# Graph attention scores: four row tiles of 32 rows instead of two of 64, with a plain key tile and a second mask buffer

## The chip, the cores and the metric

The kernel runs on one core of one Trainium2 chip. The time is that of the device for one execution, in microseconds (us), as the median of several runs. The engines are named as in the profile: PE is TensorE (matmul), PEld its weight loads, DVE is VectorE, ACT is ScalarE, POOL is GpSimd, SP is SyncE, which here only issues DMA transfers.

## The reference

128 graphs of 128 nodes with 256 features go through two layers. The first is a graph attention layer (two rounds of attention over neighbours), a layer norm, a feed-forward part of width 1024 with relu and a second norm. The second layer is the one that the change touches: attention with 8 heads of 32 features, in which each relation of the adjacency matrix has its own values.

```python
q = (src @ Wq + bq).reshape(Bb, Nn, h, dh).transpose(0, 2, 1, 3)
k = (src @ Wk + bk).reshape(Bb, Nn, h, dh).transpose(0, 2, 1, 3)
scores = jnp.einsum('bhid,bhjd->bhij', q, k) / np.sqrt(dh)
attn = jax.nn.softmax(scores, axis=-1)
out = jnp.zeros_like(q)
for r in range(Wv.shape[0]):
    v_r = (src @ Wv[r] + bv[r]).reshape(Bb, Nn, h, dh).transpose(0, 2, 1, 3)
    mask = (adj_matrix == r)[:, None]
    out = out + jnp.einsum('bhij,bhjd->bhid', attn * mask, v_r)
attn_out = out.transpose(0, 2, 1, 3).reshape(Bb, Nn, Dm) @ Wo + bo
x = _ln(src + attn_out, g1, beta1)
ff = jax.nn.gelu(x @ W1 + b1, approximate=False) @ W2 + b2
return _ln(x + ff, g2, beta2)
```

Everything is in fp32. The adjacency matrix of the inputs holds zeros and ones only, so two of the four relations occur.

## The kernel before, in words

The 128 graphs are worked on in 32 groups of 4 (`G`). A group goes through five stages: `load`, `gat` (the first layer's attention), `ff0` (its feed-forward part), `att` (the second layer's attention) and `ff1`. Each stage is a Python generator that yields planned durations; `layers` keeps the stages of several groups in a heap by due time, so that the work of neighbouring groups is interleaved. This order of emission is fixed on TensorE from planned time 280 on, and on SP's queue throughout (`kept`). [...]Two versions of all stages are built: `GENERAL` for any adjacency matrix, and `BINARY` for zeros and ones. A test at the start of the run chooses; with these inputs it is `BINARY`.

In `attention`, queries and keys of a whole group come from TensorE as 128x512 tiles (lines 468 and 474), for each of two halves of the features (`DC` = 2); 128 features are four heads of 32 (`HC` = 4). DVE writes the queries to `qT`. The keys go to a tile `kbd` that holds each key twice, in two column blocks. A column of ones and zeros (`c.own`) is the scale of the ACT instruction, and zeroes in each block the 32-row strips of every other head (line 476):

```python
for q in range(2):
    nc.scalar.activation(c.kbd[i][:, :, q], p, AF.Identity, scale=c.own[:, q:q + 1],
                         bias=c.bk_own[q][:, i:i + 1])
```

So one product over 64 rows (two heads) and 256 columns gives the scores of both heads. `weights(b)` makes for graph `b` four such products (line 490), in two row tiles of the array, into two banks of PSUM with four heads each. Then, for each bank: DVE takes the maxima (line 496), ACT the four exponentials with their sums (line 500), DVE the reciprocals (line 501), POOL scales (line 502). `turned(b)` transposes the result: DVE transposes 32x32 blocks (line 288), SP issues four DMA writes to `zd` (line 291) and one read back to `eT` (line 293); the features of a stage take the same way. `by_relation` multiplies `eT` with the mask into `m` (line 515, DVE), `values` makes `v` (lines 531 and 532), `weighted` takes the products of `eT` and `m` with `v` into `av` (line 544) in four column tiles, and line 577 applies `wo`.

In a group the scores of graphs 0 and 1 are emitted ahead of the loop over graphs, those of 2 and 3 inside it, after `weighted`. In the order on TensorE, the scores of graph 1 follow those of graph 0 with only one `av` product of the group before between them.

[...]Seven serve all tiles named `mm` (`bufs["mm"]` = 7), among them the score tiles; one serves `av`. Which bank a tile gets is settled when the program is built, and a product into a bank waits until the last reader of the tile before is done.

The other lines that matter: 333 and 378 are the products of the two halves of a feed-forward part, 346 to 360 the ACT, DVE and POOL steps between them, 403 to 407 the row of the first attention that goes out and back by DMA (`zs`, `zsd`), 435 to 454 the products of that attention.

Of the kernel before, what the change touches and what calls it, by code (L numbers as in the profile page):

```python
# [12 lines left out]
F32 = mybir.dt.float32  # L13
I32 = mybir.dt.int32
U32 = mybir.dt.uint32
AF = mybir.ActivationFunctionType
OP = mybir.AluOpType
AX = mybir.AxisListType
# [6 lines left out]
P = 128  # L25
G = 4
Q = 32
# [17 lines left out]

BINARY = dict(
    binary=True, times=TIMES,
    period=100, bufs=dict(T=5, tok=5, m=1, mm=7, v=2),
    begin=dict(load=-87, gat=-51, ff0=48, att=132, ff1=300),
    early={  # L50
        (1, "ff0"): 48,
# [34 lines left out]
def constants(tc, a, c, cst, tmp, ps):  # L86

    nc = tc.nc
    D, DC, R, MW = c.D, c.DC, c.R, c.MW
    T = G * P  # L90
    c.ident = cst.tile([P, P], F32, name="ident")
    make_identity(nc, c.ident)
    c.mhalf = cst.tile([P, G], F32, name="mhalf")
    nc.vector.memset(c.mhalf, -0.5)

    def wload(name, t=None):

        k, m = a[name].shape
        if t is None:
            t = cst.tile([P, k // P, m], F32, name=name)  # L100
        nc.sync.dma_start(t, a[name].rearrange("(c p) m -> p c m", p=P))
        return t

    def on_all_rows(first, n):

        v = a["rows"]
        return bass.AP(tensor=v.tensor, offset=v.offset + first * D, ap=[[0, P], [1, n * D]])

    c.xt, c.at = [], []

    def load_group(g):
        c.xt.append(tmp.tile([P, DC, T], F32, name=f"xt{g}"))
        nc.sync.dma_start(c.xt[g], a["xT"][g])

    def load_mask(g):
        c.at.append(tmp.tile([P, G, P], I32, name=f"at{g}"))
        nc.sync.dma_start(c.at[g], a["adjT"][g])

    m = wload("M", tmp.tile([P, DC, MW], F32, name="m_in"))
    w2T = wload("W2T", tmp.tile([P, DC, D], F32, name="w2T"))  # L120
    load_group(0)
    w1T = wload("W1T", tmp.tile([P, DC, D], F32, name="w1T"))
    load_mask(0)
    load_group(1)
    load_mask(1)

    pa = ps.tile([P, DC, 2], F32, name="mm")
    for kc in range(DC):
        for oc in range(DC):
            nc.tensor.matmul(pa[:, kc], w2T[:, oc, ts(kc, P)], m[:, oc, D:D + 2], start=oc == 0, stop=oc == DC - 1)  # L130
    nc.vector.tensor_copy(m[:, :, D:D + 2], pa)
    c.wx = cst.tile([P, DC, MW], F32, name="wx")
    for fc in range(DC):
        p = ps.tile([P, MW], F32, name="mm")
        for kc in range(DC):
            nc.tensor.matmul(p, w1T[:, kc, ts(fc, P)], m[:, kc], start=kc == 0, stop=kc == DC - 1)
        nc.vector.tensor_copy(c.wx[:, fc], p)

    for g in range(LEAD):
        nc.sync.dma_start(c.y[g], a["x"][g])  # L140
    col = cst.tile([P, a["cols"].shape[1]], F32, name="col")
    nc.sync.dma_start(col, a["cols"])
    c.col = {k: col[:, i:i + n] for k, (i, n) in COLS.items()}
    c.wf1 = wload("wf1")

    def others():

        ln_rows = cst.tile([P, len(KS), 2, D], F32, name="ln_rows")
        nc.sync.dma_start(ln_rows, on_all_rows(0, 8))
        plus = tmp.tile([P, 3, D], F32, name="plus")  # L150
        nc.sync.dma_start(plus, on_all_rows(8, 3))
        nc.vector.tensor_add(ln_rows[:, :3, 1], ln_rows[:, :3, 1], plus)
        c.ln = {k: (ln_rows[:, n, 0], ln_rows[:, n, 1]) for n, k in enumerate(KS)}
        c.wf2 = wload("wf2")
        c.wq = wload("wq")
        c.wk = wload("wk")
        c.wv = wload("wv")
        c.bv = cst.tile([P, R * D], F32, name="bv")
        nc.sync.dma_start(c.bv, on_all_rows(11, R))
        c.wo = wload("wo")  # L160
        c.w1 = wload("w1")
        c.w2 = wload("w2")
        c.kbd = [cst.tile([P, G, 2, P], F32, name=f"kbd{n}") for n in range(DC)]
        c.own = cst.tile([P, 2], F32, name="own")
        nc.vector.memset(c.own, 0.0)
        for q in range(P // Q):
            nc.vector.memset(c.own[ts(q, Q), q % 2:q % 2 + 1], 1.0)
        c.bk_own = [cst.tile([P, DC], F32, name=f"bk{q}") for q in range(2)]
        c.sums = {n: [cst.tile([P, w.shape[-1] // 2], F32, name=f"{n}s{i}") for i in (1, 2, 4)]
                  for n, w in (("wf1", c.wf1), ("w1", c.w1))}  # L170

    return others
# [43 lines left out]
def per_row(v, n):  # L216

    return v[:, :, None].to_broadcast([P, v.shape[-1], n])


def stages_of(tc, a, out, c, pools, plan):

    nc = tc.nc
    TIMES, binary = plan["times"], plan["binary"]
    ld, wk, sm, ps, dr = pools.ld, pools.wk, pools.sm, pools.ps, pools.dr
    x, xT, adjT = a["x"], a["xT"], a["adjT"]
    NG, N, _, D = x.shape
    assert N == P
    T = G * N
    NQ = N // Q  # L230
    DC, R, MW = c.DC, c.R, c.MW
    FC = a["wf1"].shape[1] // P
    H = 8
    DH = D // H
    HC = P // DH
# [223 lines left out]
    def attention(y, g, first, direct):  # L459
# [4 lines left out]
        qT = t_tile().rearrange("p (c t) -> p c t", c=DC)  # L464
        for i in range(DC):
            p = ps.tile([P, T], F32, name="mm")
            for f in range(DC):
                nc.tensor.matmul(p, c.wq[:, f, ts(i, P)], hT[:, :, f], start=f == 0, stop=f == DC - 1)  # L468
            nc.vector.tensor_scalar(qT[:, i], p, c.col["bq"][:, i:i + 1], SCALE, op0=OP.add, op1=OP.mult)

        for i in range(DC):
            p = ps.tile([P, G, N], F32, name="mm")
            for f in range(DC):
                nc.tensor.matmul(p, c.wk[:, f, ts(i, P)], hT[:, :, f], start=f == 0, stop=f == DC - 1)  # L474
            for q in range(2):
                nc.scalar.activation(c.kbd[i][:, :, q], p, AF.Identity, scale=c.own[:, q:q + 1],
                                     bias=c.bk_own[q][:, i:i + 1])

        if not binary:
            adj = ps.tile([P, G, N], F32, name="adj", bufs=1)  # L480
# [2 lines left out]
        def weights(b):  # L483


            scores = [ps.tile([P, DC, 2, N], F32, name="mm") for _ in range(2)]
            for i in range(DC):
                for h in range(2):
                    rows = ts(h, P // 2)
                    nc.tensor.matmul(scores[h][:, i], qT[rows, i, ts(b, N)], c.kbd[i][rows, b],  # L490
                                     start=True, stop=True, tile_position=(h * P // 2, 0))
            e = wk.tile([P, H, N], F32, name="e1")
            for h, p in enumerate(scores):
                p = p.rearrange("p c q n -> p (c q) n")
                nm = sm.tile([P, HC], F32, name="nm1")
                nc.vector.tensor_reduce(nm, p, AX.X, OP.max, negate=True)  # L496
                s = sm.tile([P, HC], F32, name="s1")
                eh = e[:, ts(h, HC)]
                for q in range(HC):
                    nc.scalar.activation(eh[:, q], p[:, q], AF.Exp, bias=nm[:, q:q + 1], accum_out=s[:, q:q + 1])  # L500
                nc.vector.reciprocal(s, s)  # L501
                nc.gpsimd.tensor_mul(eh, eh, per_row(s, N))  # L502
            return e

        def turned(e):
# [30 lines left out]
        def weighted(ms, v):  # L536

            po = ps.tile([P, DC, N], F32, name="av", bufs=1)

            order = range(RV) if binary else range(RV - 1, -1, -1)  # L540
            for i in range(DC):
                for n, r in enumerate(order):
                    for q in reversed(range(HC)):
                        nc.tensor.matmul(po[ts(q, DH), i], v[:, r, i * P + q * DH:i * P + (q + 1) * DH],  # L544
                                         ms[r][:, q // 2 * HC + i * 2 + q % 2],
                                         start=n == 0, stop=n == RV - 1, tile_position=(0, q * DH))
            oT = wk.tile([P, DC, N], F32, name="oT")
            nc.scalar.copy(oT, po)
            return oT
# [12 lines left out]
        v, ms = values(0), by_relation(0, eT[0], range(R))  # L562
# [36 lines left out]
def layers(ctx: ExitStack, tc: tile.TileContext, a: dict, out: bass.AP, c, plan: dict):  # L599
# [21 lines left out]
    def stage_attention(g):  # L621
        if g == 0:
            folded(nc, c, pools.ps, c.wq, c.col["bq"], "02")
            folded(nc, c, pools.ps, c.wk, c.col["bk"], "02")
            for q in range(2):
                nc.vector.tensor_scalar(c.bk_own[q], c.col["bk"], c.own[:, q:q + 1], None, op0=OP.mult)
            folded(nc, c, pools.ps, c.wv, c.bv, "02", rows=True)
            if plan["binary"]:
                D = c.D
                nc.vector.tensor_sub(c.wv[:, :, D:2 * D], c.wv[:, :, D:2 * D], c.wv[:, :, :D])  # L630
                nc.vector.tensor_sub(c.bv[:, D:2 * D], c.bv[:, D:2 * D], c.bv[:, :D])
            folded(nc, c, pools.ps, c.w1, c.col["b1"], "11")
            c.w1_sums = weight_sums(nc, c, c.w1, "w1")
        x2[g] = yield from attention(x1.pop(g), g, g == 0, g == NG - 1)
# [148 lines left out]
```

## Time and profile before

| | |
|---|---|
| median of 3 runs | 2890.71 us (2889.82 to 2892.4) |
| the profiled execution's own time | 2891.83 us |
| its span | 2890.0 us |
| mean TensorE clock granted | 0.982 |
| TensorE busy | 2787.7 us, 96% |
| ACT, POOL, DVE busy | 60%, 55%, 52% |
| scores on TensorE (L490) | 1024 records, 147.7 us busy |
| keys on ACT (L476) | 128 instructions, 92.6 us |
| exponentials on ACT (L500) | 1024 instructions, 362.1 us, with 242.9 us of reading the sums |
| maxima on DVE (L496) | 256 instructions, 162.9 us, 676 ns each |

A row of the profile names line, engine, operation, `out<-in` by the program's names, the shapes, how many there were, the busy time and the mean of one, and then the idle time of the engine ahead of it and what ended it. An fp32 product is two passes, so it shows as two records. Records of TensorE that start 7 ns apart run at the same time in different tiles of the array.

### The profile page before, as it was taken

The numbers are of one execution on the slowest core, as the hardware profiler recorded it, in microseconds if no ns is written. First come the engines' busy times: TensorE is split into PE (matmuls) and PEld (weight loads), VectorE is DVE, ScalarE is ACT, GpSimd is POOL, SyncE is SP. The second block draws the span as 40 slices with busy tenths as digits, with TensorE's granted clock in tenths as the row PEclk, the third lists the DMA queues.
The fourth block names the chain that finished last, engine by engine and source line by source line (L and its number), as shares of the span: only waits on it lengthen the run. The fifth ranks groups of instructions, "written<-read, shape, count | busy, mean of one in ns | idle before, by whom it ended". The sixth has DMA issues, their size and how long they took to land.

```text
span 2890.0 us, 45554 instructions
## 1 busy us (share of the span) xinstructions
PE 2787.7 (96%) x15554; PEld 2166.1 (75%) x15554; DVE 1504.7 (52%) x3072; ACT 1724.3 (60%) x5191; POOL 1597.4 (55%) x1866
## 2 busy tenths in 40 slices
PE   4996999999999999999999999999999999999988
PEld 3764777777877777777777787777778777777756
DVE  5444545545545555554554555555565545555442
ACT  3445566566666666666656666666666675666543
POOL 1434556556655556665655665565566565556553
PEclk7998999999999999999999999999999999999999
DMA  7145454555554556555445545454654544564310
GB/s 275 45 104 121 104 118 106 110 132 127 119 114 107 113 117 139 114 119 118 106 108 131 129 113 125 104 111 117 137 128 107 123 106 111 122 135 106 77 37 15
DMA packets 1156945, 328.69 MB, mean 114 GB/s; under 512 B 903008, under 2 KB 1126752, under 8 KB 1156064
## 3 DMA queue, kind: packets, MB, share of 16 engines
q1 hardware_dynamic: 1156704, 325.68, 49.1%
q8 instruction: 126, 2.06, 0.3%
q14 instruction: 115, 0.94, 0.1%
HBM read 195.97 MB, written 129.62 MB: 113 GB/s over the span
## 4 chain that ended last, share of the span: by engine, by line
PE 71%; DMA 7%; DVE 6%; POOL 5%; ACT 4%; issue 2%; SPq 2%; DVEq 0%; POOLq 0%; ACTq 0%
PE mm L378 25%; PE mm L333 19%; PE mm L531 5%; PE mm L474 4%; PE mm L468 4%; PE mm L490 4%; PE av L544 3%; PE mm L435 3%; PE mm L577 3%; POOL tok L271 2%; DMA zd<-e 2%; SPq L291 2%; DMA eT<-zd 2%; PE mm L454 1%; DMA zd<-T 1%
## 5 line engine op out<-in xcount | busy, mean ns | idle before, releaser
L271 POOL TENSOR_TENSOR tok<-tok,ln_rows 128x512 f32<-128x512 f32 (+1 forms) x596 | 669.5, 1133 | 34.4 <-PE mm L282 11.1
L500 ACT ACTIVATE e<-mm,nm 128x128 f32<-128x128 f32 x1024 | 362.1, 397 | 239.2 <-DVE nm L496 229.6
L378 PE MATMUL mm<-w,fT 128*128 128x256 f32 x2048 | 460.6, 381 | 0.0
L378 PE MATMUL mm<-wf,fT 128*128 128x256 f32 x2048 | 456.6, 381 | 1.5 <-ACT fT L354 1.5
L378 PEld LDWEIGHTS mm<-w,fT 128*128 128x128 f32 x2048 | 386.6, 190 | 74.2 <-issue 24.2
L502 POOL TENSOR_TENSOR e<-e,s 128x512 f32<-128x512 f32 x256 | 269.4, 1053 | 300.5 <-DVE s L501 299.8
L378 PEld LDWEIGHTS mm<-wf,fT 128*128 128x128 f32 x2048 | 386.5, 190 | 64.3 <-issue 9.2
L515 DVE TENSOR_TENSOR m<-eT,am 128x1024 f32<-128x1024 f32 x128 | 186.2, 1454 | 385.2 <-DMA eT<-zd 374.8
L496 DVE TENSOR_REDUCE nm<-mm 128x4 f32<-128x512 f32 x256 | 162.9, 676 | 254.6 <-PE mm L490 254.6
L265 ACT ACTIVATE tok<-tok,nmr,rstd 128x256 f32<-128x256 f32 x480 | 249.9, 603 | 20.1 <-POOL nmr L263 20.0
L531 PE MATMUL mm<-wv,T 128*128 128x512 f32 x512 | 249.3, 610 | 0.0
L352 POOL TENSOR_TENSOR fT<-fT 128x512 f32<-128x512 f32 x128 | 163.3, 1277 | 153.8 <-ACT fT L351 153.8
L500 ACT ACTIVATION_READ_ACCUMULATOR e<-mm,nm 128x1 f32 x1024 | 242.9, 237 | 0.0
L354 ACT ACTIVATE fT<-fT,col 128x512 f32<-128x512 f32 x256 | 170.4, 715 | 118.8 <-DVE fT L348 117.1
L309 POOL TENSOR_TENSOR t<-T 128x256 f32<-128x256 f32 x64 | 47.6, 744 | 321.3 <-DMA T<-zd 321.0
L333 PE MATMUL mm<-T,w 128*128 128x256 f32 x768 | 202.3, 386 | 4.0 <-DMA T<-zd 2.9
L424 POOL TENSOR_TENSOR e<-e,s 128x512 f32<-128x512 f32 (+1 forms) x68 | 68.1, 1002 | 244.4 <-DVE s L423 230.6
L333 PE MATMUL mm<-T,wf 128*128 128x256 f32 x768 | 193.1, 381 | 0.0
L256 DVE BATCH_NORM_STATS2 st<-tok 128x6 f32<-128x256 f32 x480 | 176.7, 409 | 2.4
L333 PEld LDWEIGHTS mm<-T,w 128*128 128x128 f32 x768 | 144.4, 192 | 30.6 <-issue 6.5
L422 ACT ACTIVATE e<-e,nm 128x128 f32<-128x128 f32 x256 | 101.6, 430 | 105.2 <-DVE nm L419 98.8
L333 PEld LDWEIGHTS mm<-T,wf 128*128 128x128 f32 x768 | 146.1, 191 | 21.7 <-issue 0.8
(144 smaller groups left out, 5147.1 us busy)
## 6 DMA issues: line engine op xcount, KB each, us to landing
zd<-e SPq DMA_DIRECT2D x496, 128.0 KB, 4.6
eT<-zd SPq DMA_DIRECT2D x124, 512.0 KB, 4.4
zd<-T SPq DMA_DIRECT2D x364, 128.0 KB, 3.5
T<-zd SPq DMA_DIRECT2D x91, 512.0 KB, 4.2
xt<-in_xT_dram SPq DMA_DIRECT2D x32, 512.0 KB, 5.0
e<-zsd SPq DMA_DIRECT2D x60, 256.0 KB, 3.3
tok<-in_x_dram SPq DMA_DIRECT2D x30, 512.0 KB
out_dram<-tok SPq DMA_DIRECT2D x29, 512.0 KB, 5.4
```

The source lines that it names most:

```text
L256: nc.vector.bn_stats(st, y[:, b])
L265: nc.scalar.activation(y[:, b], y[:, b], AF.Identity, bias=nmr[:, b:b + 1], scale=rstd[:, b:b + 1])
L271: engine.tensor_tensor(y[:, b:b + n], y[:, b:b + n], v[:, None, :].to_broadcast([P, n, D]), op)
L333: nc.tensor.matmul(p[:, i], win[k][:, ts(f0 + i, P)], hs[k], start=first and i == 0, stop=True, skip_group_check=True)
L352: nc.gpsimd.tensor_add(hi[:, :, 1], hi[:, :, 1], hi[:, :, 0])
L354: nc.scalar.activation(lo[:, i], lo[:, i], func, bias=bin_[:, f0 + i:f0 + i + 1])
L378: nc.tensor.matmul(ys[b // 2][:, b % 2], fT[f][:, ts(b, N)], wout[:, f], start=b % 2 == 0 and n == 0, stop=n == FC - 1, skip_group_check=True)
L496: nc.vector.tensor_reduce(nm, p, AX.X, OP.max, negate=True)
L500: nc.scalar.activation(eh[:, q], p[:, q], AF.Exp, bias=nm[:, q:q + 1], accum_out=s[:, q:q + 1])
L502: nc.gpsimd.tensor_mul(eh, eh, per_row(s, N))
L515: nc.vector.tensor_tensor(m, eT, at[:, b][:, None, :].to_broadcast([P, H, N]), OP.mult)
L531: nc.tensor.matmul(p, hT[:, b, f], wv[:, f, r:r + 2], start=f == 0, stop=f == DC - 1)
```

## The change

`kbd` and what belongs to it go. The keys are written once, with their bias, to a plain tile `kT` of the same layout as `qT`. The scores of a graph are eight products over 32 rows (one head) and 128 columns, in four row tiles, and each row tile writes to a bank of its own: four banks with two heads each instead of two with four. Maxima are taken for each bank; reciprocals and the scaling on POOL still for four heads at a time. The order of heads in `e` changes, and `weighted` reads it in the new order. In `BINARY` the mask product `m` has two buffers instead of one.

```diff
-    period=100, bufs=dict(T=5, tok=5, m=1, mm=7, v=2),
+    period=100, bufs=dict(T=5, tok=5, m=2, mm=7, v=2),
...
-        c.kbd = [cst.tile([P, G, 2, P], F32, name=f"kbd{n}") for n in range(DC)]
-        c.own = cst.tile([P, 2], F32, name="own")
-        nc.vector.memset(c.own, 0.0)
-        for q in range(P // Q):
-            nc.vector.memset(c.own[ts(q, Q), q % 2:q % 2 + 1], 1.0)
-        c.bk_own = [cst.tile([P, DC], F32, name=f"bk{q}") for q in range(2)]
...
+        kT = wk.tile([P, DC, T], F32, name="kT", bufs=1)
         for i in range(DC):
-            p = ps.tile([P, G, N], F32, name="mm")
+            p = ps.tile([P, T], F32, name="mm")
             for f in range(DC):
                 nc.tensor.matmul(p, c.wk[:, f, ts(i, P)], hT[:, :, f], start=f == 0, stop=f == DC - 1)
-            for q in range(2):
-                nc.scalar.activation(c.kbd[i][:, :, q], p, AF.Identity, scale=c.own[:, q:q + 1],
-                                     bias=c.bk_own[q][:, i:i + 1])
+            nc.scalar.activation(kT[:, i], p, AF.Identity, bias=c.col["bk"][:, i:i + 1])
...
-            scores = [ps.tile([P, DC, 2, N], F32, name="mm") for _ in range(2)]
+            scores = [ps.tile([P, DC, N], F32, name="mm") for _ in range(HC)]
             for i in range(DC):
-                for h in range(2):
-                    rows = ts(h, P // 2)
-                    nc.tensor.matmul(scores[h][:, i], qT[rows, i, ts(b, N)], c.kbd[i][rows, b],
-                                     start=True, stop=True, tile_position=(h * P // 2, 0))
+                for q in range(HC):
+                    rows = ts(q, DH)
+                    nc.tensor.matmul(scores[q][:, i], qT[rows, i, ts(b, N)], kT[rows, i, ts(b, N)],
+                                     start=True, stop=True, tile_position=(q * DH, 0))
             e = wk.tile([P, H, N], F32, name="e1")
-            for h, p in enumerate(scores):
-                p = p.rearrange("p c q n -> p (c q) n")
-                nm = sm.tile([P, HC], F32, name="nm1")
-                nc.vector.tensor_reduce(nm, p, AX.X, OP.max, negate=True)
-                s = sm.tile([P, HC], F32, name="s1")
-                eh = e[:, ts(h, HC)]
-                for q in range(HC):
-                    nc.scalar.activation(eh[:, q], p[:, q], AF.Exp, bias=nm[:, q:q + 1], accum_out=s[:, q:q + 1])
-                nc.vector.reciprocal(s, s)
-                nc.gpsimd.tensor_mul(eh, eh, per_row(s, N))
+            nm = sm.tile([P, H], F32, name="nm1")
+            s = sm.tile([P, H], F32, name="s1")
+            for h in range(2):
+                some = slice(h * HC, (h + 1) * HC)
+                for q in (2 * h, 2 * h + 1):
+                    nc.vector.tensor_reduce(nm[:, ts(q, DC)], scores[q], AX.X, OP.max, negate=True)
+                for q in (2 * h, 2 * h + 1):
+                    for i in range(DC):
+                        k = q * DC + i
+                        nc.scalar.activation(e[:, k], scores[q][:, i], AF.Exp, bias=nm[:, k:k + 1],
+                                             accum_out=s[:, k:k + 1])
+                nc.vector.reciprocal(s[:, some], s[:, some])
+                nc.gpsimd.tensor_mul(e[:, some], e[:, some], per_row(s[:, some], N))
...
-                                         ms[r][:, q // 2 * HC + i * 2 + q % 2],
+                                         ms[r][:, q * DC + i],
```

More of the change, by code (lines that the diff above doesn't have):

```diff
@@ L624, in stage_attention @@
             folded(nc, c, pools.ps, c.wk, c.col["bk"], "02")
-            for q in range(2):
-                nc.vector.tensor_scalar(c.bk_own[q], c.col["bk"], c.own[:, q:q + 1], None, op0=OP.mult)
             folded(nc, c, pools.ps, c.wv, c.bv, "02", rows=True)
```

## The prediction

> **What bounds the kernel now.** I read the shares of busy time first, then the table by stage, then the instructions of one group in order of time, and last the chain that ended last.
>
> The table by stage has, after the stretch, its length, then busy time (and instructions) of PE, weight loads, DVE, ACT and POOL, the clock, DMA share and GB/s:
>
> ```profile
> PE 2787.7 (96%) x15554; PEld 2166.1 (75%) x15554; DVE 1504.7 (52%) x3072; ACT 1724.3 (60%) x5191; POOL 1597.4 (55%) x1866
> ...
> 288.00:2760.00 2472.00, 2460.93 (x13887) 1919.25 (x13886) 1322.57 (x2705) 1544.53 (x4660) 1452.67 (x1684) 1.00 0.52 116
> ```
>
> From 288 to 2760 us TensorE is busy 99.6% of the time at full clock; ACT, DVE and POOL have 37% to 47% free. The groups follow each other there every 85.05 us (14 of 26), 85.2 us (7) or 85.7 to 85.8 us (5). So a microsecond that TensorE saves or loses in a group counts, unless something else takes its place. The start (0 to 288) and the end are different: PE is busy 219.7 of the first 288 us.
>
> Now the place that the change touches, TensorE, then ACT, then DVE around one pair of scores (start, length, line, operation):
>
> ```profile
> 1581.49 1.13 PE L490 MATMUL mm<-kbd,T 64*128 64x256 f32 x8
> 1582.56 0.42 PE L544 MATMUL av<-eT,v 128*32 128x128 f32 x8
> ...
> 1583.57 1.13 PE L490 MATMUL mm<-kbd,T 64*128 64x256 f32 x8
> 1584.63 0.70 PE L378 MATMUL mm<-w,fT 128*128 128x256 f32 x2
> ```
> ```profile
> 1583.38 0.37 ACT L500 ACTIVATE e<-mm,nm 128x128 f32<-128x128 f32 x1 [5.94 <-DVE nm L496]
> ...
> 1585.11 0.39 ACT L500 ACTIVATE e<-mm,nm 128x128 f32<-128x128 f32 x1
> 1585.36 0.23 ACT L500 ACTIVATION_READ_ACCUMULATOR e<-mm,nm 128x1 f32 x1
> ```
> ```profile
> 1582.66 1.29 DVE L496 TENSOR_REDUCE nm<-mm 128x4 f32<-128x512 f32 x2 [6.35 <-PE mm L490]
> ```
>
> One graph's scores hold TensorE for 1.06 us (1582.56 - 1581.49). Graphs 0 and 1 of a group stand almost back to back, with one `av` product (1.01 us) between. The exponentials of graph 0 start 1.89 us after its first product and go at 0.34 us each; the sixth is done at 1585.59.
>
> The chain, last. It leaves TensorE at 1507.55 and comes back at 1560.60:
>
> ```profile
> 1508.42 1.24 DVE e L288
> ...
> 1524.15 4.42 DMA zsd<-zs
> ...
> 1531.93 4.24 DMA zd<-T
> ...
> 1559.37 0.71 ACT fT L354
> 1560.08 0.48 ACT fT L346
> ...
> 1560.60 1.13 PE mm L333 x4
> ```
>
> Transposes go out and back by DMA, one round trip after the other in SP's queue[...]. I took, in all 26 steady groups, the time between the end of L346's copy and the product L333 that waits for it: 0.05 us in 11 groups, about 1.1 us in 4, 1.8 to 2.3 us in 11. So this second bound stands level with TensorE in 11 groups of 26 and just behind in the others. Between 1507.55 and 1560.60 lie the scores of graphs 2 and 3 (1523.96 and 1542.62); those of 0 and 1 lie outside.
>
> [...]two row tiles start 7 ns apart, and a block of scores costs 0.2 us more than its four passes of 0.216 us. [...]load time goes with the columns, not the rows; the trace agrees: 187 ns for 64x128 (L490) and 190 for 128x128, against 110 for 128x32 (L544). So rows of 32 make no load cheaper. [...]
>
> **The change part by part.**
>
> *Score products.* Four passes of 256 columns (two row tiles at a time) become four of 128 columns (four at a time). A 128-column pass takes 0.109 us in L544. So 4 x 0.109 + 0.20 = 0.64 us, 0.42 less per graph. [...]Not concurrent at all: 1.94. I take 0.64, since column tiles of this size do reach 0.109.
>
> *Banks.* Seven banks serve `mm`; two graphs now ask for eight. The changed kernel's list of instructions has the order on TensorE from 288 us on unchanged, and shows that graph 1's second, third and fourth tiles use the banks of graph 0's first, second and third, so they wait for graph 0's second, fourth and sixth exponential. Count from graph 0's first product. Its results come 0.42 us sooner: DVE starts at 1.17 - 0.42 = 0.75. A maximum over 128x256 takes 0.41 (L419 has that form), and an exponential now waits for its own bank's maximum alone: ACT starts at 0.75 + 0.41 + 0.04 = 1.20. The sixth exponential with its accumulator is done 2.21 after that (1585.59 - 1583.38): 3.41. TensorE takes 0.05 to notice (as at 1560.60) and then a block of 0.64: it is free at 4.10, where before it was at 3.14. The pair **loses 0.96 us**; 0.87 if the bank is free at the exponential itself[...]. All of TensorE's queue stands behind it: L378, then the step at 1507.55 + 85.2 from which the DMA chain starts. So it is paid in full.
>
> *Graphs 2 and 3.* Their banks are free a microsecond or more before: they save 2 x 0.42 = 0.84 us of TensorE, inside the stretch that the chain spans. In 11 of 26 groups TensorE would only wait longer for L346 and nothing is gained; in 15 it is.
>
> *Key tile.* Four activations of 0.774 us per group become two: 64 x 0.774 = 50 us less of ACT. Covered: they end 5 us before the scores (1576.1 against 1581.5).
>
> *Maxima.* 512 x 0.408 - 256 x 0.676 = 36 us more of DVE. For graphs 2 and 3 a wait for DMA follows on DVE (3.0 us ahead of L515 at 1550.65), which hides it; for the pair it is counted above. Were the cover gone, L347 would be 0.3 us late.
>
> *Second mask buffer.* DVE waits for it once in the run, 8.0 us between 140 and 310 us; elsewhere L515 waits for the DMA of eT. Nothing in the steady part. In the start it may give up to 8 us or, since TensorE waits for another DMA there (12 us at 228), nothing. There the pair stalls too, 2 to 5 us, in idle time mostly. I take +1, bounds -6 to +6, for start and end.
>
> *Orders.* ACT's and SP's are the same over a group; DVE's and POOL's have a few neighbours exchanged. On POOL t L309 now stands behind rstd L259, so POOL's run there ends about 1.1 us later; its next reader, the transpose of e, has 5.8 us to spare. Nothing.
>
> **The sum.** 29 turns: 11/26 of them at +0.96, 15/26 at +0.96 - 0.84 = +0.12, mean 0.48: +14 us, +1 for the ends: the profiled execution's 2891.8 becomes about 2907; it stands 1.1 above the median of the three runs, so 2906.
>
> **The rivals.**
> - *TensorE alone sets the time*: the chain gives way. 29 x 0.12 = +3.5: 2894. For it: 15 groups have slack. Against: 11 have none. Chance 0.15.
> - *The chain holds in every group*: 29 x 0.96 = +28: 2919. Chance 0.10.
> - *Row tiles do not run four at a time*: 0.88 us more per graph instead of 0.42 less, and later exponentials: about +4.5 us a group, 3020. Against: two do, and four column tiles do. Chance 0.05.
> - *The bank wait is not paid* (the other side): the three banks come free before graph 1 asks for them, 1.65 us after the start. Then the pair gains 0.84 and the group 0.84 + 0.84 x 15/26 = 1.32: 2852. It decides at the time of the sixth exponential: the time falls from a release before 2.9 us on, against 3.41 worked out above. For it: ACT and DVE stand idle 6 us ahead and start at once. Against: six exponentials take 2.2 us, so the first would have to start at 0.7 instead of 1.20. Chance 0.10.
> - The forecast, chance 0.60, 2894 to 2914 by its bounds.
>
> **How the numbers follow.** What a measurement of this kernel can tell from no change is 0.2%, 5.8 us. Slower by more: most of the forecast (0.54), all of the second and third rival: 0.69. Within: 0.06 of the forecast and most of the first rival: 0.19. Faster: the last rival, and a good outcome of the start: 0.12. The range 2887 to 2922 takes in the forecast and the first two; it leaves out 0.15 and some of the edges.
>
> **What would show it.** Right: score blocks of 0.64 us for graphs 0, 2 and 3; the second block of the pair stretched to about 2.4 us, TensorE waiting for exponentials in it; 4.1 us from graph 0's product to L378; groups every 85.2 to 86.1 us. Wrong: no wait on ACT inside the second block, blocks over 0.8 us, or groups at or under 85.0 us.

## The result, and the profile after

The changed kernel takes **2914.82 us** (median of 4 runs, 2913.89 to 2915.51); the kernel before took 2891.56 beside it (4 runs, 2889.82 to 2892.98). The ratio is 1.0081, interval 1.0063 to 1.0098: slower by 0.8%. The forecast was 2906, range 2887 to 2922. The profiled execution took 2914.78 us with a span of 2913.0, against 2891.83 and 2890.0, so 23.0 us have to be found in the traces.

First the page of the kernel after: busy time of each engine, the chain that ended last, and the rows of exponentials and maxima. Below it stands the chain that ended last in the kernel before.

```profile
PE 2795.1 (96%) x16578; PEld 2181.4 (75%) x16578; DVE 1512.2 (52%) x3321; ACT 1674.8 (57%) x5127; POOL 1594.7 (55%) x1866
...
PE 85%; ACT 3%; DVE 3%; DMA 3%; issue 2%; POOL 2%; SPq 1%; ACTq 0%; DVEq 0%; POOLq 0%
...
L495 ACT ACTIVATE e<-mm,nm 128x128 f32<-128x128 f32 x1024 | 361.2, 394 | 218.8 <-DVE nm L491 209.4
...
L491 DVE TENSOR_REDUCE nm<-mm 128x2 f32<-128x256 f32 x512 | 182.6, 411 | 245.8 <-PE mm L483 245.7
```
```profile
PE 71%; DMA 7%; DVE 6%; POOL 5%; ACT 4%; issue 2%; SPq 2%; DVEq 0%; POOLq 0%; ACTq 0%
```

ACT has lost 50 us of work and a block of scores that waits for nothing is shorter on TensorE (below), yet the kernel is longer: neither saving reached the end. A maximum over 256 columns takes 0.411 us, as assumed. TensorE's share of the chain went from 71% to 85% and that of DMA from 7% to 3%, so the place to look is TensorE.

The pair of scores in one group, TensorE, then ACT, then DVE (start, length, line, operation, number of passes, and in brackets the idle time before it and who ended it). A block of eight products is sixteen passes (L483 has 2048 records for 1024 products):

```profile
1588.63 0.73 PE L483 MATMUL mm<-kT,T 32*128 32x128 f32 x16
1589.29 0.43 PE L540 MATMUL av<-eT,v 128*32 128x128 f32 x8
...
1590.30 0.88 PE L483 MATMUL mm<-kT,T 32*128 32x128 f32 x4
1591.39 0.48 PE L483 MATMUL mm<-kT,T 32*128 32x128 f32 x2 [0.21 <-ACT e L495]
1592.09 0.71 PE L483 MATMUL mm<-kT,T 32*128 32x128 f32 x10 [0.21 <-ACT e L495]
1592.72 3.72 PE L372 MATMUL mm<-w,fT 128*128 128x256 f32 x16
```
```profile
1589.83 0.37 ACT L495 ACTIVATE e<-mm,nm 128x128 f32<-128x128 f32 x1 [6.01 <-DVE nm L491]
...
1591.56 0.39 ACT L495 ACTIVATE e<-mm,nm 128x128 f32<-128x128 f32 x1
1591.81 0.23 ACT L495 ACTIVATION_READ_ACCUMULATOR e<-mm,nm 128x1 f32 x1
```
```profile
1589.37 1.41 DVE L491 TENSOR_REDUCE nm<-mm 128x2 f32<-128x256 f32 x4 [4.46 <-PE mm L483]
```

The first block, free of waits, holds TensorE for 0.66 us (1589.29 - 1588.63; before 1.06). The second, with as many passes, takes 2.42 us (1592.72 - 1590.30): it waits twice for an exponential of the graph before. The brackets show only 0.21 us each, since the modelled ends of the products ahead cover the rest; the distance between the starts shows the wait. The sixth exponential ends at 1592.04 with its accumulator, and the next product starts at 1592.09.

The chain over the same group (start, length, what):

```profile
1504.81 0.23 ACT e L495
1505.04 0.04 issue
1505.09 0.71 PE mm L483 x10
...
1552.55 5.12 DMA eT<-zd
...
1567.21 0.48 ACT fT L340
1567.69 0.04 issue
1567.73 1.13 PE mm L327 x4
```

It now runs through the exponentials that free the bank (1504.81) and then along TensorE until 1552.53. Before, it left TensorE ahead of this stretch and came back 53 us later; here it is away for 15 us. The round trips by DMA have less say in this group than the prediction gave them.

The steady stretch, in the columns of the table by stage:

```profile
288.00:2730.00 2442.00, 2419.90 (x14509) 1895.11 (x14508) 1301.08 (x2887) 1467.77 (x4519) 1413.22 (x1640) 1.00 0.52 115
```

TensorE is busy 99.1% of it, 99.6% before. The clock is 1.00 when rounded, but not everywhere. Two groups, each with the stretch of 3.41 us in which the second block starts and the 3.41 us after it:

```profile
1245.69:1249.10 3.41, 2.98 (x28) 2.17 (x21) 1.61 (x7) 3.41 (x20) 2.15 (x3) 1.00 0.01 5
1249.10:1252.51 3.41, 3.41 (x10) 2.69 (x9) 2.73 (x7) 3.41 (x20) 1.52 (x2) 0.50 0.00 0
1590.43:1593.84 3.41, 2.98 (x21) 2.27 (x22) 1.61 (x8) 3.41 (x19) 3.41 (x5) 1.00 0.31 73
1593.84:1597.25 3.41, 3.41 (x18) 3.00 (x17) 3.16 (x8) 3.41 (x21) 1.40 (x2) 1.00 0.02 5
```
```profile
1248.25 5.41 PE L372 MATMUL mm<-w,fT 128*128 128x256 f32 x16
1253.49 1.03 PE L327 MATMUL mm<-T,wf 128*128 128x256 f32 x4
```

In the first group TensorE gets **half its clock** (0.50) from 1249.10 to 1252.51, and the sixteen passes of L372 last 5.24 us (1253.49 - 1248.25). Those at 1592.72 last 3.56 (the next line starts at 1596.28). That is 1.68 us that no wait shows. It happens in 5 of the 26 steady groups, and in none before. This was in no term of my sum.

Where the 23.0 us went, by the trace: the start -1.5, the 26 groups +19.3, the end +5.2. A group takes 85.98 us on the mean, against 85.24. Of the 19.3, 5.5 is the longer group without any other wait (85.26 against 85.05, so 26 x 0.21), 8.4 the five half-clock stretches (5 x 1.68), and the 5.4 that remain are other waits (10.2 after, 4.8 before). As far as the records show them, they are for the last steps of the DMA chain (L340, L341), with idle time in 12 cases after and in none before, and in four or five cases on each side for `v`. The end holds two more half-clock stretches, at 2686.1 and 2713.4 us; the kernel before has none there until 2801. At the same 1.68 us each, an estimate, they would be 3.4 of its 5.2 us.

### The profile page after: what moved, and what is told of

The parts are those of the page before. It is cut to its first block, busy times and chain, and to the rows that moved or that the text cites. A ratio compares the mean times of both kernels' runs of the same rounds, so it can differ in the third digit from the quotient of the medians.

```text
span 2913.0 us, 47820 instructions
## 1 busy us (share of the span) xinstructions
PE 2795.1 (96%) x16578; PEld 2181.4 (75%) x16578; DVE 1512.2 (52%) x3321; ACT 1674.8 (57%) x5127; POOL 1594.7 (55%) x1866
## 4 chain that ended last, share of the span: by engine, by line
PE 85%; ACT 3%; DVE 3%; DMA 3%; issue 2%; POOL 2%; SPq 1%; ACTq 0%; DVEq 0%; POOLq 0%
PE mm L372 31%; PE mm L327 24%; PE mm L527 7%; PE mm L462 4%; PE mm L469 4%; PE mm L573 3%; PE mm L483 3%; PE av L540 3%; PE mm L429 3%; ACT e L495 2%; PE mm L448 2%; PE mm L437 2%; DMA eT<-zd 1%; DMA zd<-e 1%; DVE nm L491 1%
## 5 line engine op out<-in xcount | busy, mean ns | idle before, releaser
L372 PE MATMUL mm<-w,fT 128*128 128x256 f32 x2048 | 471.2, 387 | 0.0
L372 PE MATMUL mm<-wf,fT 128*128 128x256 f32 x2048 | 458.2, 381 | 1.5 <-ACT fT L348 1.5
L372 PEld LDWEIGHTS mm<-w,fT 128*128 128x128 f32 x2048 | 393.4, 193 | 71.1 <-issue 14.5
L372 PEld LDWEIGHTS mm<-wf,fT 128*128 128x128 f32 x2048 | 384.4, 190 | 61.6 <-ACT fT L354 5.0
L491 DVE TENSOR_REDUCE nm<-mm 128x2 f32<-128x256 f32 x512 | 182.6, 411 | 245.8 <-PE mm L483 245.7
L253 POOL TENSOR_SCALAR rstd<-mv 128x4 f32<-128x4 f32 x129 | 32.0, 248 | 261.9 <-DVE mv L251 256.6
L382 DVE TENSOR_TENSOR tok<-tok,mm 128x512 f32<-128x512 f32 x120 | 81.5, 679 | 165.0 <-PE mm L372 165.0
```

Of the source, the lines that this page charges most:

```text
L372: nc.tensor.matmul(ys[b // 2][:, b % 2], fT[f][:, ts(b, N)], wout[:, f], start=b % 2 == 0 and n == 0, stop=n == FC - 1, skip_group_check=True)
L491: nc.vector.tensor_reduce(nm[:, ts(q, DC)], scores[q], AX.X, OP.max, negate=True)
```

## The experiments

Two theories. The **bank wait**: the second block waits for the exponentials because the two graphs ask for eight of seven banks, and that costs more than the row tiles save; half clock follows from the same wait. The **rivals**: the row tiles cost something themselves; or the second mask buffer, the key tile or the many small maxima do; or the DMA chain sets the time whatever TensorE saves.

**Later scores.** The scores of graph 1 stand behind eight more products of L372, so that exponentials have time; the next planned step (`turn0`) is shortened by as much, so that what follows keeps its planned time. Tiles, banks and counts stay.

```
-    binary=True, times=TIMES,
+    binary=True, times=TIMES | dict(scores=7, turn0=8.5),
```

> The changed kernel, with the scores of graph 1 emitted later in planned time (7 instead of 5.5), so that on TensorE eight products of the feed-forward part (3.5 us) stand between the av product and them; nothing else moves in a steady group. Theory (the cost is the wait of the pair for banks): the sixth exponential of graph 0 is done 3.41 us after its first product, graph 1 asks at 0.66 + 1.01 + 3.5 = 5.2 us, so no wait is left; four blocks of 0.66 us, groups every 83.5 us where the DMA chain does not hold and 84.3 where it does, and no stretch at half clock in the steady part: 2850 us (2840 to 2866). Rival (row tiles of 32, the smaller maxima or the DMA chain cost the time, not the wait): 2890 to 2915 us.

Measured: 2881.87 us (2876.0 to 2882.32), ratio to before 0.9957, interval 0.9943 to 0.9971. TensorE in one group:

```profile
1567.52 0.73 PE L483 MATMUL mm<-kT,T 32*128 32x128 f32 x16
...
1572.84 0.73 PE L483 MATMUL mm<-kT,T 32*128 32x128 f32 x16
1573.50 1.13 PE L327 MATMUL mm<-T,wf 128*128 128x256 f32 x4
...
1596.80 6.31 PE L372 MATMUL mm<-wf,fT 128*128 128x256 f32 x28 [0.35 <-ACT fT L354]
```

Both blocks of the pair now take 0.66 us, and between 288 and 2640 us no half clock is left: with the bank wait, both losses are gone. But the time is 32 us above what I expected, in neither range. A new wait for ACT (0.35 us in the last line, 0.5 to 0.6 us of TensorE's time) comes in nearly every group, since ACT does graph 1's exponentials later; that they are what delays it is read from the trace, not tested. Waits of other kinds come back in nine or ten groups. A typical group takes 84.34 us, the mean 84.73. About half of what was set free was taken by the next in line.

**Four banks without row tiles of 32.** The kernel before, its 64-row products cut into 128 columns, so that a graph writes to four banks, with maxima for each bank as in the change; the doubled key tile and the one mask buffer stay.

```
-            scores = [ps.tile([P, DC, 2, N], F32, name="mm") for _ in range(2)]
+            scores = [ps.tile([P, DC, N], F32, name="mm") for _ in range(HC)]
...
+                for q in range(2):
+                    for h in range(2):
+                        rows = ts(h, P // 2)
+                        nc.tensor.matmul(scores[2 * h + q][:, i], qT[rows, i, ts(b, N)], c.kbd[i][rows, b, q],
```

> The kernel before (doubled key tile, row tiles of 64, one mask buffer), with the products cut into 128 columns and each head pair in a bank of its own: four banks as in the change, without its faster products. Theory: a block stays at 1.07 us (8 passes of 0.109 and 0.2), graph 1 waits for the sixth exponential of graph 0, which is done about 3.65 us after the first product; L378 starts at about 4.5 us instead of 3.14. Nothing is saved elsewhere: +1.4 us a group, 2930 to 2945 us. Rival (the bank wait is not what costs): 2891 us, or the 2915 us of the change if its banks and not its products set the time.

Measured: 2939.2 us (2937.55 to 2940.07), ratio 1.016, interval 1.0143 to 1.0177. TensorE:

```profile
1602.56 0.67 PE L491 MATMUL mm<-kbd,T 64*128 64x128 f32 x4
1603.44 0.49 PE L491 MATMUL mm<-kbd,T 64*128 64x128 f32 x2 [0.21 <-ACT e L503]
1604.14 0.93 PE L491 MATMUL mm<-kbd,T 64*128 64x128 f32 x10 [0.21 <-ACT e L503]
1605.00 1.35 PE L378 MATMUL mm<-w,fT 128*128 128x256 f32 x5
```

Waits for the same exponentials, 2.44 us for the block (1605.00 - 1602.56), without one 32-row tile. The banks make them. Of the 2.44 us, 1.35 are waiting, since TensorE itself works 1.09 us on such a block. There is no half clock between 288 and 2700 us. The change is 24 us faster than this: its blocks of 0.66 us, against 1.09 here (1601.55 - 1600.46 in the same group), earn back part of what the banks cost.

**One bank fewer.** The changed kernel with six banks for `mm`.

```
-    period=100, bufs=dict(T=5, tok=5, m=2, mm=7, v=2),
+    period=100, bufs=dict(T=5, tok=5, m=2, mm=6, v=2),
```

> The changed kernel with six banks for the products instead of seven (one bank stays unused). Graph 1 of each group then waits for the second, fourth, sixth and eighth exponential of graph 0 with its four tiles. Theory: two exponentials more are 0.69 us a group, L372 starts 4.8 us after the first product instead of 4.09; +20 us for 29 groups, and more stretches at half clock[...]: 2932 to 2955 us. Rival (the pair is hidden by the DMA chain, or costs by its products): 2915 us.

Measured: 3015.1 us (3009.7 to 3027.2), ratio 1.0433, interval 1.0402 to 1.0463. TensorE in a group without half clock and in one with it:

```profile
748.56 0.73 PE L483 MATMUL mm<-kT,T 32*128 32x128 f32 x16
...
753.35 3.72 PE L372 MATMUL mm<-w,fT 128*128 128x256 f32 x16
```
```profile
1562.60 0.48 PE L483 MATMUL mm<-kT,T 32*128 32x128 f32 x2 [0.33 <-ACT e L495]
...
1564.69 1.22 PE L483 MATMUL mm<-kT,T 32*128 32x128 f32 x10 [0.21 <-ACT e L495]
1565.84 6.48 PE L372 MATMUL mm<-w,fT 128*128 128x256 f32 x16
```

The direction and the 0.7 us of wait were right: in the first of these groups L372 starts 4.79 us after the first product (753.35 - 748.56; 4.8 was expected). The time is 60 us above the range. The trace has 27 half-clock stretches between 288 and 2730 us, three of them of double length. At 1.7 us each (1.68 in the changed kernel), an estimate, they are at least 46 us. 23 of them follow the waits of the second block, four a wait of 2.7 us of L437 for L528, the reader of another product's bank. Such waits for other banks make up most of the rest: this first group, which takes 87.63 us though it has no half clock, has a wait of L437 of 1.5 us. So with the longer wait this kernel has more half clock (27 stretches, against 7 of the changed kernel in the same stretch of time), and this costs more than what was added to the wait (29 x 0.70 = 20 us).

**One mask buffer.** The changed kernel with `m=1`.

```
-    period=100, bufs=dict(T=5, tok=5, m=2, mm=7, v=2),
+    period=100, bufs=dict(T=5, tok=5, m=1, mm=7, v=2),
```

> The changed kernel with one mask buffer, as before. The wait for it on DVE showed once in the run before, 8.0 us in the start. Theory: no difference that can be measured, 2915 us (2910 to 2919). Rival (the second buffer lets the masks run ahead and hides part of the loss): 2920 us or more.

Measured: 2913.07 us (2906.56 to 2919.57), ratio 1.0072, interval 1.0047 to 1.0098. Not to be told from the changed kernel: no effect of the second buffer can be seen. The profiled execution, at 2910.05 us, has three half-clock stretches in its 26 steady groups instead of five, with the same blocks and the same waits.

**Early scores.** The changed kernel, with graph 0's scores in the middle of sixteen products (32 passes) of L372; graph 1's stay behind these.

```
-    binary=True, times=TIMES,
+    binary=True, times=TIMES | dict(qk=1, scores=9),
...
-        yield TIMES["ff first half"]
+            if b == 1:
+                yield 3
+        yield TIMES["ff first half"] - 3
```

> The changed kernel with the scores of graph 0 emitted earlier, in the middle of the sixteen products of the feed-forward part that stand ahead of them; graph 1 keeps its place. ACT is idle there, so graph 0's exponentials go into idle time instead of delaying later ACT work as they do where graph 1 is moved back. Theory (bank wait, then ACT and DMA waits take what it frees): no wait in the pair, blocks of 0.66 us, the wait of the second feed-forward product for ACT after graph 2's scores (0.5 to 0.6 us a group with graph 1 moved back) shrinks to 0.1; groups every 83.6 to 84.3 us; 2845 to 2868 us, no stretch at half clock. Rival (chain of DMA round trips alone eats what is freed): 2870 to 2885, like graph 1 moved back.

Measured: 2871.81 us (2866.19 to 2876.38), ratio 0.993, interval 0.9912 to 0.9949: **the fastest version here**, ahead of both kernels. TensorE:

```profile
469.64 0.73 PE L485 MATMUL mm<-kT,T 32*128 32x128 f32 x16
470.30 3.72 PE L372 MATMUL mm<-w,fT 128*128 128x256 f32 x16
473.95 0.43 PE L542 MATMUL av<-eT,v 128*32 128x128 f32 x8
...
474.96 0.73 PE L485 MATMUL mm<-kT,T 32*128 32x128 f32 x16
475.61 3.72 PE L372 MATMUL mm<-w,fT 128*128 128x256 f32 x16
```

Between the first products of the two blocks lie 5.32 us (474.96 - 469.64), not 1.67 (1590.30 - 1588.63), and every block takes 0.66. No half clock occurs between 275 and 2770 us. The group takes 83.69 or 83.70 us in 13 of 26 cases; the others are longer by 0.5 to 1.9 us, with waits for DVE and ACT steps of the DMA chain (L341, L340) or for `v`, so the mean is 84.24. The time lies 4 us above my range for that reason and inside the rival's, that the chain eats what is freed. It is also 10 us less than with graph 1 moved back, and the records show no wait of L372 for L354 any more. By these traces that wait was part of the loss there, and the chain is part of it here.

**The same order without row tiles.** The kernel before with the two edits of the last experiment.

> The kernel before in the same order on TensorE (scores of graph 0 in the middle of the sixteen products). A control: there is no bank wait to take away. Theory: products of 64 rows stay at 1.06 us, nothing is freed: 2891 us (2884 to 2896). Rival (the new order itself gives the gain, by ACT): 2880 us or less.

Measured: 2901.12 us (2897.26 to 2903.96), ratio 1.0025, interval 1.0015 to 1.0036. The order brings nothing by itself, rather 0.2% of loss (5 us above my range, away from the rival's). In this order the usual group takes 85.25 us with the old scores and 83.69 with the row tiles: 1.56 less, where four blocks of 0.40 make 1.60. So the row tiles are worth what their blocks say, once nothing waits.

**A slower chain.** The kernel before with three small extra loads a group on SP, ahead of a step of the round trips.

```
+            if k == D:
+                for n in range(3):
+                    nc.sync.dma_start(sm.tile([P, 1], F32, name=f"more{n}"), x[0][:, 0, n:n + 1])
```

> The kernel before with three more DMA transfers of 128 x 4 bytes issued on SP's queue in each steady group, ahead of the row of the second attention round, in the stretch that the chain of DMA round trips spans; they cost SP's queue about 0.5 us each. Theory (that chain is level with TensorE in 11 of 26 groups and 1.1 and 1.8 to 2.3 us behind in the others): a chain 1.5 us longer costs 1.5 us in 11 groups, 0.4 in 4 and nothing in 11: +0.7 us a group, +20 us: 2911 us (2900 to 2925). Rival (TensorE alone sets the time): 2891 us.

Measured: 2902.49 us (2900.82 to 2905.22), ratio 1.0033, interval 1.0019 to 1.0047. SP's own queue in one group:

```profile
1530.45 1.38 SPq L406 DMA_DIRECT2D more<-in_x_dram  x3
1531.87 0.54 SPq L408 DMA_DIRECT2D zsd<-zs  x1
```

The loads take 1.38 us of the queue (0.46 each) and a group is 0.40 us longer on the mean (85.63 against 85.24). The chain has a say, so the rival that TensorE alone sets the time falls; but a delay of the chain is passed on by less than a third. The measured time lies at the lower end of the range (2900 to 2925), about half-way between the theory's 2911 and the rival's 2891.

**The plain key tile alone.** The kernel before with one key tile instead of the doubled one. The two heads of a row tile are summed in its scores.

```
-        c.kbd = [cst.tile([P, G, 2, P], F32, name=f"kbd{n}") for n in range(DC)]
...
+            nc.scalar.activation(kT[:, i], p, AF.Identity, bias=c.col["bk"][:, i:i + 1])
...
-                    nc.tensor.matmul(scores[h][:, i], qT[rows, i, ts(b, N)], c.kbd[i][rows, b],
+                    nc.tensor.matmul(scores[h][:, i], qT[rows, i, ts(b, N)], kT[rows, i, ts(b, N)][:, None, :].to_broadcast([P // 2, 2, N]),
```

> The kernel before with the plain key tile alone: two ACT instructions per group instead of four; the products keep 64 rows and 256 columns in two banks and read the key tile twice, so that the two heads of a row tile are added instead of kept apart (that part of the computation is left out). Theory: 50 us less of ACT, all of it hidden: 2891 us (2886 to 2895). Rival (ACT's time counts): 2880 us or less.

Measured: 2893.72 us (2888.57 to 2897.31), ratio 1.0001, interval 0.9993 to 1.001. The 50 us of ACT that it saves are hidden.

## Why the prediction was right

- **Score products: right.** 0.64 us worked out, 0.66 measured. That four row tiles run at once was my estimate, from two row tiles and four column tiles; now the records of L483 show it, four of them 7 ns apart. Against sixteen passes of 0.109 one after the other (1.74) the block is 2.6 times as fast; once the 0.20 of fixed cost is taken off (an estimate, 1.06 - 4 x 0.216 in the kernel before), which leaves 0.46, some 3.8 times. A load of 32 rows takes 188 ns (L483), one of 64 rows 187 (L490): no cheaper, as assumed.
- **Banks: right, step by step.** Counted from graph 0's first product at 1588.63: DVE starts at 0.74 (worked out 0.75), ACT at 1.20 (1.20), the sixth exponential is done at 3.41 (3.41), L372 starts at 4.09 (4.10). The rival that the bank wait is not paid needed a release before 2.9.
- **Key tile and second mask buffer: right.** One alone gives a ratio of 1.0001, leaving out the other gives 1.0072 beside 1.0081.
- **Maxima: nearly right.** 20 us more of DVE busy time, not 36, as DVE's neighbouring records overlap (L491 is busy 182.6 us, its 512 x 0.411 are 210); by count and length (512 x 0.411 less 256 x 0.676) it is 37. I didn't test them by themselves; the fastest version has all 512 of them.
- **The group without other waits: too small.** +0.12 us worked out, +0.21 measured: the blocks of graphs 2 and 3 give 2 x 0.40 and not 2 x 0.42, and L372 now waits a little for ACT's L354. Over 26 groups that is 5.5 us, not 3.1. That L354 takes the rest is read from the trace, not tested.
- **The chain: right in kind, too large.** I let graphs 2 and 3 save nothing in 11 of 26 groups, which is 0.84 x 11 = 9.3 us; all waits beyond the usual group, the chain's among them, grew by 5.4. The slowed chain shows why the share must be less than whole: 1.38 us of delay gave 0.40.
- **The step that was missing: the clock.** The sum priced TensorE's wait at its own length. The trace shows 8.4 us more in five groups, where the wait is followed by a half-clock stretch. The other differences nearly cancel, which is chance: 2.4 more for the longer group, 3.9 less for the chain, 2.7 more at start and end (+3.7 measured, +1 assumed; the two half-clock stretches of the end are in it), 1.4 less for the three turns that I counted beyond the 26. So the measured time lies inside the range by its width, 8 us above the sum's 2907, and not because the clock was foreseen. The two experiments without the wait have one such stretch and none between 288 and 2730 us; the one with a longer wait has 27.

The criteria came out so: blocks of 0.66, a second block of 2.42, 4.09 us to L372, waits on ACT inside the block. From one second block to the next it is 85.26 or 85.27 us in 12 of 27 groups and 85.8 in five, inside the stated 85.2 to 86.1; ten take 86.3 to 88.0 and lie outside, among them the five with half clock.

## What to carry to other kernels

Here products cut into four tiles that run at once asked for four banks instead of two, so two graphs asked for eight of seven. (Both kernels give each row tile banks of its own; that they have to was not shown.) Before counting what such a cut saves, count banks over neighbouring uses, and put the release of the first bank (first product, maximum, exponentials, one by one) on the clock against the next use. If they collide, separate the two uses by other work: here the same row tiles are 0.8% slower back to back and 0.7% faster with 3.6 us more between. And look at the granted clock in windows of a few us around a wait of TensorE: after a wait of 1.76 us here it cost another 1.68 in five of 26 groups.

## What the hardware showed that I had not expected

From 288 to 2730 us TensorE is busy 99.1% of the time, and yet it lost half its clock there seven times (0.50). These drops of the changed kernel last 3.413 us each, and their distances are multiples of that (1075.0, 1249.1, 1764.5, 1938.6 and 2112.7 us in the steady part: 51, 151, 51 and 51 times; then 2686.1 and 2713.4: 168 and 8 times). So I divided the time, counted from a drop, into stretches of 3.413 us, here called windows. For the 28 second blocks from 380 us on I took where in its window each starts. The kernel with one mask buffer, whose blocks are the same, fills the gap that the changed kernel leaves. Its two cases next to the edge (second blocks at 2446.97 and 2532.24 us), each with its window and the next:

```profile
2446.03:2449.44 3.41, 2.98 (x50) 2.18 (x49) 1.60 (x6) 2.93 (x17) 1.04 (x1) 1.00 0.00 0
2449.44:2452.86 3.42, 3.42 (x17) 3.03 (x17) 3.39 (x9) 3.42 (x18) 1.38 (x2) 1.00 0.02 5
2531.37:2534.78 3.41, 2.98 (x49) 2.18 (x45) 1.62 (x6) 3.00 (x17) 1.04 (x1) 1.00 0.00 0
2534.78:2538.19 3.41, 3.41 (x9) 2.66 (x10) 3.38 (x9) 3.41 (x18) 1.44 (x2) 0.50 0.01 2
```

All of them:

```
start of the second block in its window     groups   half clock in the next window
changed kernel        0.12 to 0.43 us         6           6
                      1.40 us or later       22           0
one mask buffer       0.25 to 0.87 us         3           3
                      0.94 to 1.21 us        10           0
                      1.42 us or later       15           0
```

The sixth of the changed kernel (2710 us) lies behind the 26 steady groups. So in these two runs the edge lies between 0.87 and 0.94 us. A block of 2.43 us that starts at 0.94 still ends inside its window of 3.41 and is spared, so it is not enough that the whole wait lies inside one window. With six banks, where the wait is longer, the drop came up to a start at 1.70 us; from 1.74 on it didn't. The group of 85.26 us is almost 25 windows (85.33), so from one usual group to the next the position moves by only 0.07 us, and a good one lasts long. In the changed kernel no two neighbouring groups have a drop: from a second block with one it is 86.8 to 88.0 us to the next, which so starts elsewhere in its window (1.69 us or later).

The traces show two rates, 0.50 and 1.00, and short waits for banks went ahead of all nine drops in the table. TensorE waited there for some 1.76 of the 3.41 us (2.42 - 0.66), and by the records, whose ends are modelled, for only 0.43.

What stays open is what in the wait brings the drop. The kernel with four banks and 64-row products has blocks of the same length at 0.11 to 0.81 us in eight groups and no drop in them. It waits less in each (1.35 us, against 1.76), as its own work takes longer, and its products use twice the rows. Either may be the reason; no run here separates the two.
